# Two fused graph layers on one core: layer 0's masks kept on chip for layer 1, most loads moved to other steps and given one buffer

## The chip, the cores and the metric

The kernel runs on one core of a Trainium2 chip. A core has a matmul engine (PE, with its weight loads shown apart as PEld), a vector engine (DVE), a scalar engine (ACT), a general engine (POOL) and a queue processor (SP) that here only issues DMAs. Each of them works through its own list of instructions in order; a semaphore wait at the head of a list holds up everything behind it. Sixteen DMA engines move the data. The metric is the device time of one execution, in microseconds (us), lower is better.

## The reference

The input is `x`, 16 graphs of 1024 nodes with 256 features, and `adj`, 16 x 1024 x 1024 integers, here only zeros and ones (about 3% ones).

```
# layer 0: attention with 8 heads of 32, masked by adj == 0
h = relu(layernorm(x))
Q, K, V = h @ Wq.T + bq, h @ Wk.T + bk, h @ Wv.T + bv
scores = Q K.T * 32**-0.5, -inf where adj == 0
x = x + (softmax(scores) V) @ Wo.T + bo
# layer 1: one score per edge, by the kind of the edge (adj = 1, 2, 3, 4)
h = relu(layernorm(x))
e_k = leaky_relu((h * a_k) @ h.T, 0.2)
scores = e_0 where adj == 1, e_1 where adj == 2, ..., -9e15 elsewhere
x = x + softmax(scores) @ h
```

With an `adj` of zeros and ones, layer 1 needs e_0 alone. The kernel computes that case in its main loop, finds out on the way whether any graph has other values, and has a branch that computes layer 1 again for such a graph (`layer_1_of_kinds`, L597). With this input the branch is not entered.

## The kernel before, in words

The work is cut into 128 tiles: 16 graphs (b) of 8 tiles (t) of 128 rows. One pass of the main loop is a **step** s; it has eight parts, h = 0 to 7, one for each head of layer 0. Three kinds of objects are in flight:

- `Attend(b, t)` is layer 0 for one tile. In step s the object `now` has tile s: for each head h, `scores(h)` (PE, L402), `softmax_max(h)` (DVE, L414, adds the mask to the scores and finds the row's maximum), one part later `softmax_exp(h-1)` (ACT, L422), and one more part later the probabilities of head h-2 are turned over so that they can be multiplied by the values. For odd heads PE transposes and ACT copies (`turn`, L514, L515). For heads 0, 2, 4 and 6 (`BY_BLOCKS`) DVE transposes 32 x 32 blocks (`turn_blocks`, L347) and four DMAs of 128 KB put the blocks in place (`place_blocks`, that is `placed`, L352). `combine(0)` at h = 7 multiplies heads 0 to 3 by the values, `combine(1)`, at h = 3 of the next step (the object is then called `was`), heads 4 to 7 (PE, L457). So head 6's blocks, which are placed at h = 0, have to be in place by h = 3. I write place(6) for those four DMAs.
- `Edges(b, t)` is layer 1 for one tile, LAG = 9 steps behind layer 0. `prepare` (POOL, L530) scales a tile of h by a_0, `score(0)` and `score(1)` at h = 0 and 1 make the scores (PE, L543), `softmax_max` at h = 2 adds the mask and finds the maximum (DVE, L556), `leak`, `softmax_exp`, `turn_blocks` and `place_blocks` follow until h = 6, and in the step after that `gather` (PE, L584) and `store` (DVE, L593, and the DMA of the result).
- `Piece(b, t)` is layer 0's projection for a tile of the next graph, 9 steps ahead: load of x (`xin`, L192), layernorm statistics (`stats`, DVE, at h = 7), the scale by a Newton iteration on POOL (`scaled`, L144 to L160), `normed`, transposes, projections, and keys and queries written to DRAM (`kd`, `qd`). The main loop is preceded by a **start** that does this for the eight tiles of graph 0 with two large pieces of four tiles each, and for one small one.

What bears on the change:

- The mask. `Attend.mask` (POOL, L384, at h = 3 for the next tile) turns the 128 x 1024 integers into a bf16 tile `neg` with -1e30 where adj is 0. `Edges.mask` (POOL, L537, at h = 7 for the next tile) does the same from a second load of the same rows. Layer 0's load reads the rows in a "mixed" order over the partitions (`mixed`, L342: row 32b + k of the tile goes to partition 4k + b), which the block transposes make necessary; layer 1's load reads them in plain order. Each load is 512 KB.
- The flag. `Attend.flag` (ACT, L393) squares adj - 0.5 in place and sums, which tells whether there is anything but 0 and 1. It runs at h = 0 for the current tile and ends the use of the integers.
- The DMAs. SP issues nearly all of them in program order. In the order of a step: h = 0: keys of the piece (`kd`, L297), place(6); h = 1: `kd`, the next tile's adj (L376), the next tile's queries `qt` (L372); h = 2: place(0); h = 3: `xin` (L192), layer 1's adj (L525); h = 4: place(2), x1 for `store` (L572, issued in `Edges.softmax_exp`); h = 6: queries of the piece (`qd`, L291), place(4), `x1d` (L486, layer 0's result to DRAM), `xb` (L380, the residual's input), layer 1's four placing DMAs; h = 7: the result (L594). POOL issues a second copy of the keys at h = 1, and around a change of graph the eight loads of the next graph's keys, 512 KB each (`load_key`, L331): five in step t = 7 and three in step t = 0.
- `work.tile(...)` takes a buffer from a ring for its tag; the tags had two buffers unless told otherwise. A tile whose ring is full waits for the last reader of the oldest.

Of the kernel before, what the change touches and what calls it, by code (L numbers as in the profile page):

```python
# [8 lines left out]
F32 = mybir.dt.float32  # L9
# [33 lines left out]
def gnn_kernel(  # L43
# [25 lines left out]
    LAG = NT + 1  # L69
    LEAD = NT + 1  # L70

    const = ctx.enter_context(tc.tile_pool(name="const", bufs=1))
# [98 lines left out]
    class Piece:  # L171
# [5 lines left out]
        def __init__(self, b, first, n=1):  # L177
            self.b, self.first, self.n = b, first, n
            self.cols = slice(first * P, (first + n) * P)
            self.projected, self.halved, self.again = [], [], []  # L180
            self.tags = ("xin", "h0", "hT", "halves", "hTm") if n == 1 else ("adj", "pT", "qt", "p", "blocks")

        def buffer(self, i, shape, dtype=F32, bufs=2):
# [79 lines left out]
        def high(self):  # L263
            which, oc, ps, bias = self.projected.pop(0)
            halves = self.buffer(3, [P, 2 * self.n * P], F32R, 4)
# [91 lines left out]

    h1s, h1Ts, x1ds = {}, {}, {}
    kinds_seen = const.tile([P, B * NT], F32, name="kinds_seen")

    class Attend:


# [10 lines left out]
        def load(self):  # L374
            self.adj = work.tile([P, N], I32, tag="adj")
            nc.sync.dma_start(out=self.adj, in_=mixed(adj[self.b, self.rows, :]))  # L376

        def load_nodes(self):
            self.xb = work.tile([P, D], F32, tag="xb")
            nc.sync.dma_start(out=self.xb, in_=mixed(x[self.b, self.rows, :]))  # L380

        def mask(self):
            self.neg = work.tile([P, N], BF16, tag="neg")
            nc.gpsimd.tensor_scalar(self.neg, self.adj, 0.0, MASKED, ALU.is_equal, ALU.mult)  # L384
            self.sums = small.tile([P, HEADS], F32, tag="sums")
# [79 lines left out]
        def combined(self):  # L465
            self.oT = work.tile([P, NC, P], F32, tag="oT")
            nc.vector.tensor_tensor(self.oT, by_chunk(sums_place), self.recT, ALU.mult)
# [8 lines left out]
        def residual(self):  # L476
            self.x1 = work.tile([P, D], F32, tag="x1")
            nc.vector.tensor_tensor(self.x1, self.y, self.xb, ALU.add)
            mv = small.tile([P, 1, nc.vector.BN_AGGR_DIM], F32, tag="mv1")
            stats_of(self.x1, mv[:, 0, :])  # L480
            self.norm = norm_of(mv, 1, "1")

        def keep(self):
            if self.t == 0:
                x1ds[self.b] = dram.tile([N, D], F32, tag=f"x1d{self.b}", name=f"x1d_{self.b}", bufs=1)
            nc.sync.dma_start(out=mixed(x1ds[self.b][self.rows, :]), in_=self.x1)  # L486

# [30 lines left out]
    class Edges:  # L518
# [3 lines left out]

        def load(self):
            self.adj = work.tile([P, N], I32, tag="adj")
            nc.sync.dma_start(out=self.adj, in_=adj[self.b, self.rows, :])  # L525

        def prepare(self):
            self.ha = work.tile([P, NC, P], F32, tag="ha")
            for c in range(NC):
                nc.gpsimd.tensor_scalar(  # L530
                    self.ha[:, c], h1Ts[self.b][:, c, self.rows], a_t[:, c, 0:1], 0.0, ALU.mult, ALU.add
                )

        def mask(self):
            self.neg = work.tile([P, N], BF16, tag="neg1", bufs=1)

            nc.gpsimd.tensor_scalar(self.neg, self.adj, 0.0, MASKED, ALU.is_equal, ALU.mult)  # L537

# [12 lines left out]


        def softmax_max(self):
            self.sel = work.tile([P, N], F32, tag="sel", bufs=1)
            top = small.tile([P, 1], F32, tag="top")
            nc.vector.tensor_tensor_reduce(  # L556
                out=self.sel, in0=self.e, in1=self.neg, scale=-1.0, scalar=3e38,
                op0=ALU.add, op1=ALU.min, accum_out=top,
            )
            self.nmx = small.tile([P, 1], F32, tag="nmx1")  # L560
            nc.vector.scalar_tensor_tensor(self.nmx, top, SLOPE, top, ALU.mult, ALU.min)
# [4 lines left out]
        def softmax_exp(self):  # L566
# [3 lines left out]
            )  # L570
            self.x1 = work.tile([P, D], F32, tag="x1b")
            nc.sync.dma_start(out=self.x1, in_=x1ds[self.b][self.rows, :])  # L572
# [16 lines left out]
        def store(self):  # L589
            rec = small.tile([P, 1], F32, tag="rec1")  # L590
            nc.vector.reciprocal(rec, self.total)
            ot = work.tile([P, D], F32, tag="ot")
            nc.vector.scalar_tensor_tensor(ot, sums_place, rec, self.x1, ALU.mult, ALU.add)  # L593
            nc.sync.dma_start(out=out[self.b, self.rows, :], in_=ot)  # L594


    def layer_1_of_kinds(b):  # L597
        h1 = graph.tile([P, NT, D], F32, tag="h1", name=f"h1g_{b}")
        h1T = graph.tile([P, NC, N], F32, tag="h1T", name=f"h1Tg_{b}")
        for t in range(NT):  # L600
            rows = slice(t * P, (t + 1) * P)
            xt = work.tile([P, D], F32, tag="x1")
            nc.sync.dma_start(out=xt, in_=x1ds[b][rows, :])
            mv = small.tile([P, 1, nc.vector.BN_AGGR_DIM], F32, tag="mv1")
# [7 lines left out]
        for t in range(NT):  # L612
            rows = slice(t * P, (t + 1) * P)
            at = work.tile([P, N], I32, tag="adj")
            nc.sync.dma_start(out=at, in_=adj[b, rows, :])
            xt = work.tile([P, D], F32, tag="x1b")
            nc.sync.dma_start(out=xt, in_=x1ds[b][rows, :])

            code = work.tile([P, N], BF16, tag="neg1", bufs=1)
            nc.gpsimd.tensor_scalar(code, at, 5.0, 0.0, ALU.min, ALU.max)  # L620
            sel = work.tile([P, N], F32, tag="sel", bufs=1)
            nc.vector.memset(sel, NEG_INF)
            for k in range(N_KINDS):
                ha = work.tile([P, NC, P], F32, tag="ha")
# [4 lines left out]
                is_k = work.tile([P, N], U16, tag="neg")  # L629
                nc.vector.tensor_scalar(is_k, code, float(k + 1), None, ALU.is_equal)  # L630
# [21 lines left out]
            nc.vector.reciprocal(rec, total)  # L652
            ot = work.tile([P, D], F32, tag="ot")
            nc.vector.scalar_tensor_tensor(ot, o, rec, xt, ALU.mult, ALU.add)
# [19 lines left out]
    with tc.manual_schedule():  # L674
# [35 lines left out]
        for s in range(B * NT + LAG + 1):  # L710
            b, t = divmod(s, NT)
            nxt, edge_nxt, piece_nxt = attend_of(s + 1), edges_of(s + 1), piece_of(s + 1)
            for h in range(HEADS):
# [41 lines left out]
                if h == 0:  # L755
                    if edge:
                        edge.score(0)
                    if gone:
                        gone.turn_normed()
                        gone.turned_normed()  # L760
                    if now:
                        now.flag()
                if h == 1:
# [8 lines left out]
                    if nxt:  # L772
                        nxt.load()
                        nxt.load_queries()
# [28 lines left out]
                if h == 5:  # L803
# [37 lines left out]
                if now and h < 3 and t == 0 and b > 0:  # L841
                    load_key(b, HEADS - 3 + h)
            gone, was, now = was, now, nxt
            edge_was, edge = edge, edge_nxt
# [53 lines left out]
```

## Time and profile before

| | |
|---|---|
| time, median of 3 runs | 3405.14 us (3405.12 to 3412.75) |
| the profiled execution: its own time, its span | 3404.83 us, 3403.0 us |
| PE, DVE, ACT, POOL busy | 3126.6, 2788.1, 2418.2, 2432.1 us |
| mean granted PE clock | 0.978 |
| DMA | 830.24 MB, 244 GB/s on average |
| masks of layer 0 on POOL (L384) | 128 x 3653 ns |
| masks of layer 1 on POOL (L537) | 128 x 3659 ns |
| loads of adj, both layers | 256 of 512 KB, 5.3 us from issue to landing (median) |

A step in the middle of a graph takes about 24.6 us. "Idle before" an instruction is time in which its engine stood still, and the arrow names what ended it; the releaser is inferred, so that among several it can be a neighbour of the true one. The chain of work that ended last covers only the last 30 us of this run: it is followed back from the last instruction and breaks off where no releaser is recorded. Records of PE overlap, because matmuls are pipelined.

### The profile page before, as it was taken

The page shows a single profiled execution, that of the slowest core. Times are in us where ns is not written, and L with a number is a line of the kernel's source. Part 1 is how long each engine was busy: PE and PEld are TensorE (multiplying, and loading weights), DVE is VectorE, ACT ScalarE, POOL GpSimd, SP SyncE. Part 2 cuts the span into 40 slices and gives each one's busy share as a digit, 9 for nine tenths or more (in the row PEclk, how much of TensorE's full clock was granted, in tenths as well). Part 3 has the DMA queues.
Part 4 walks back from the last instruction along what each step waited for, and adds up shares of the span by engine and source line. Part 5 has one row for each costly group of instructions (what it writes and reads, how often), then busy time and mean ns, then how long its engine had stood idle before and what let it go on. Part 6 is the DMA issues. An engine that isn't in the chain of part 4 may idle for free. (4 is left out here: it accounts for less than half of the span.)

```text
span 3403.0 us, 100938 instructions
## 1 busy us (share of the span) xinstructions
PE 3126.6 (92%) x36018; PEld 2247.9 (66%) x36018; DVE 2788.1 (82%) x5111; ACT 2418.2 (71%) x4829; POOL 2432.1 (71%) x5634
## 2 busy tenths in 40 slices
PE   5879989999999989999899999999999999998988
PEld 3666767666676767766666676767666676666653
DVE  3878888788888888888788788888888888788874
ACT  2887767677777777777777677777777677776751
POOL 2567777777777777777777777777777777776553
PEclk7999999999999999999999999999999999999999
DMA  6787788888888788788878888888788888888664
GB/s 221 211 249 241 234 268 249 268 239 245 265 241 277 236 268 247 237 271 248 267 231 250 265 236 282 240 270 248 234 268 249 267 235 251 267 238 261 196 175 113
DMA packets 802029, 830.24 MB, mean 244 GB/s; under 512 B 73840, under 2 KB 742640, under 8 KB 801520
## 3 DMA queue, kind: packets, MB, share of 16 engines
q1 hardware_dynamic: 769520, 725.10, 71.3%
q0 software_dynamic: 28800, 94.39, 7.9%
q8 instruction: 291, 4.77, 0.5%
q10 hardware_dynamic: 3200, 4.19, 0.3%
q14 instruction: 218, 1.79, 0.1%
HBM read 320.08 MB, written 167.77 MB: 143 GB/s over the span
## 5 line engine op out<-in xcount | busy, mean ns | idle before, releaser
L422 ACT ACTIVATE p<-p,nmx 128x1024 f32<-128x1024 f32 x1024 | 1179.2, 1152 | 454.9 <-DVE nmx L414 450.9
L414 DVE CUSTOM_DVE_ANT_0 p<-s,neg 128x1024 f32<-128x1024 f32 x1024 | 1242.1, 1213 | 207.2 <-PE s L402 195.8
L402 PE MATMUL s<-k,qt 128*128 128x512 f32 x2048 | 794.5, 469 | 41.3 <-DMA k<-kd 14.8
L457 PE MATMUL acc<-pT,v 128*32 128x128 f32 x16384 | 576.3, 283 | 140.2 <-DMA pT<-blocks 136.6
L515 ACT COPY pT<-trp 128x512 f32<-128x512 f32 x1024 | 542.5, 580 | 136.1 <-PE trp L514 134.6
L347 DVE STREAM_TRANSPOSE blocks<-p 128x1024 f32<-128x1024 f32 x512 | 634.8, 1240 | 0.0
L457 PEld LDWEIGHTS acc<-pT,v 128*32 128x32 f32 x16384 | 476.1, 113 | 213.6 <-issue 204.4
L514 PE MATMUL trp<-ident,p 128*128 128x128 f32 x4096 | 534.0, 274 | 2.1 <-ACT p L422 2.0
L514 PEld LDWEIGHTS trp<-ident,p 128*128 128x128 f32 x4096 | 480.7, 141 | 75.1 <-ACT p L422 6.9
L384 POOL TENSOR_SCALAR neg<-adj 128x1024 bf16<-128x1024 int32 x128 | 467.6, 3653 | 78.8 <-DMA adj<-in_adj 69.8
L584 PE MATMUL acc<-h,pT 128*32 128x256 f32 x8192 | 505.8, 383 | 6.2 <-DMA pT<-blocks 5.5
L537 POOL TENSOR_SCALAR neg<-adj 128x1024 bf16<-128x1024 int32 x128 | 468.4, 3659 | 39.0 <-DMA adj<-in_adj 29.0
L402 PEld LDWEIGHTS s<-k,qt 128*128 128x128 f32 x2048 | 328.9, 191 | 232.0 <-issue 136.6
L543 PE MATMUL s<-h1T,ha 128*128 128x512 f32 x1024 | 481.3, 593 | 0.5 <-ACT h1T L504 0.5
L584 PEld LDWEIGHTS acc<-h,pT 128*32 128x32 f32 x8192 | 244.0, 110 | 219.3 <-issue 73.2
L156 POOL TENSOR_SCALAR sq<-sq 128x1 f32<-128x1 f32 (+1 forms) x750 | 238.6, 318 | 65.5
L441 POOL COPY wide<-rec 128x256 f32<-128x256 f32 x128 | 51.1, 399 | 325.7 <-DVE rec L439 325.6
L543 PEld LDWEIGHTS s<-h1T,ha 128*128 128x128 f32 x1024 | 183.9, 190 | 141.1 <-issue 127.5
L556 DVE CUSTOM_DVE_ANT_0 sel<-s,neg 128x1024 f32<-128x1024 f32 x128 | 156.7, 1224 | 134.8 <-POOL ve L144 85.4
L157 POOL TENSOR_TENSOR r<-r,sq 128x1 f32<-128x1 f32 (+1 forms) x750 | 168.8, 225 | 62.6
L297 POOL DMA_DIRECT2D kd<-halves x240 | 176.6, 773 | 33.9 <-issue 24.3
L422 ACT ACTIVATION_READ_ACCUMULATOR p<-p,nmx 128x1 f32 x1024 | 198.7, 194 | 0.0
(103 smaller groups left out, 4096.6 us busy)
## 6 DMA issues: line engine op xcount, KB each, us to landing
pT<-blocks SPq DMA_DIRECT2D x2560, 128.0 KB, 3.3
adj<-in_adj SPq DMA_DIRECT2D x256, 512.0 KB, 5.3
qt<-qd SPq DMA_DIRECT2D x128, 512.0 KB, 5.9
qd<-halves SPq DMA_DIRECT2D x240, 256.0 KB, 3.3
k<-kd POOLq DMA_DIRECT2D x120, 512.0 KB, 7.1
kd<-halves SPq DMA_DIRECT2D x240, 128.0 KB, 2.3
kd<-halves POOLq DMA_DIRECT2D x240, 128.0 KB, 5.3
xb<-in_x SPq DMA_DIRECT2D x128, 128.0 KB, 2.5
```

The source lines that it names most:

```text
L156: g.tensor_scalar(sq, sq, 1.5, None, ALU.add)
L347: nc.vector.transpose(blocks.rearrange("p b j q -> p j b q"), p)
L384: nc.gpsimd.tensor_scalar(self.neg, self.adj, 0.0, MASKED, ALU.is_equal, ALU.mult)
L402: nc.tensor.matmul(self.ps[:, cols], lhsT=self.qt[:, h, :], rhs=keysets[self.b][h][:, cols], start=True, stop=True,)
L414: nc.vector.tensor_tensor_reduce(out=p, in0=sides[h in (3, 5, 7)], in1=self.neg, scale=-SCALE, scalar=FLOOR, op0=ALU.add, op1=ALU.min, acc ...
L422: nc.scalar.activation(p, p, AF.Exp, bias=nmx, scale=-1.0, accum_out=self.sums[:, h : h + 1])
L457: nc.tensor.matmul(sums_place[r * HD : (r + 1) * HD, g * P : (g + 1) * P], lhsT=vs[self.b][:, j, place_of(h) : place_of(h) + HD], rhs=self ...
L514: nc.tensor.transpose(tr[:, j, :], p[:, jj * P : (jj + 1) * P], ident)
L515: copy(pT[:, half * 4 : half * 4 + 4, :], tr)
L537: nc.gpsimd.tensor_scalar(self.neg, self.adj, 0.0, MASKED, ALU.is_equal, ALU.mult)
L543: nc.tensor.matmul(self.e[:, cols], lhsT=self.ha[:, c, :], rhs=h1Ts[self.b][:, c, cols], start=(c == 0), stop=(c == NC - 1),)
L584: nc.tensor.matmul(sums_place[a * HD : (a + 1) * HD, :], lhsT=self.pT[:, j, a], rhs=h1s[self.b][:, j, :], start=(j == 0), stop=(j == NT - 1),)
```

## The change

The masks of layer 0 stay on chip in a ring of `KEPT = LAG + 1 = 10` buffers, and layer 1 reads the one of its tile: `Edges.load` and `Edges.mask` are gone. Since that mask has its rows in the mixed order, layer 1 now handles its rows in that order too: `prepare` permutes the columns of its weights as it scales them, x1 goes to DRAM and comes back in mixed order as it lies, and the result is stored through `mixed`. The branch for other kinds keeps the plain order (`in_order`).

The integers of layer 0 have one buffer instead of two. They are loaded two tiles ahead, at h = 7 (`nxt2.load`), after the flag of the next tile, which moves from h = 0 of its own step to h = 6 of the step before. `xin` moves from h = 3 to h = 5, x1 (`Edges.load_nodes`) from h = 4 of the step before to h = 0 of the step of `store`, `xb` from the step before the tile's own to h = 6 of the tile's own. Nearly all other tags get one buffer. The large pieces of the start take their x from the `pT` ring, not from `adj`, and the start now flags the first tile and loads the second.

```diff
+    KEPT = LAG + 1
-            self.tags = ("xin", "h0", "hT", "halves", "hTm") if n == 1 else ("adj", "pT", "qt", "p", "blocks")
+            self.tags = ("xin", "h0", "hT", "halves", "hTm") if n == 1 else ("pT", "pT", "qt", "p", "blocks")
-            bufs = {"p": 4, "blocks": 3}.get(tag, bufs)
+            bufs = {"p": 4, "blocks": 3, "halves": 4, "qt": 2}.get(tag, 1)
...
+    def in_order(rows):
+        return rows.rearrange("(k b) n -> b k n", b=NB)
     class Attend:
         def load(self):
-            self.adj = work.tile([P, N], I32, tag="adj")
+            self.adj = work.tile([P, N], I32, tag="adj", bufs=1)
...
         def mask(self):
-            self.neg = work.tile([P, N], BF16, tag="neg")
+            self.neg = work.tile([P, N], BF16, tag="neg", bufs=KEPT)
+            masks[self.b, self.t] = self.neg
...
         def keep(self):
-            nc.sync.dma_start(out=mixed(x1ds[self.b][self.rows, :]), in_=self.x1)
+            nc.sync.dma_start(out=x1ds[self.b][self.rows, :], in_=self.x1)
     class Edges:
-        def load(self):
-            self.adj = work.tile([P, N], I32, tag="adj")
-            nc.sync.dma_start(out=self.adj, in_=adj[self.b, self.rows, :])
         def prepare(self):
-                    self.ha[:, c], h1Ts[self.b][:, c, self.rows], a_t[:, c, 0:1], 0.0, ALU.mult, ALU.add
+                    self.ha[:, c].rearrange("p (k b) -> p k b", b=NB),
+                    h1Ts[self.b][:, c, self.rows].rearrange("p (b k) -> p k b", b=NB),
+                    a_t[:, c, 0:1], 0.0, ALU.mult, ALU.add,
-        def mask(self):
-            self.neg = work.tile([P, N], BF16, tag="neg1", bufs=1)
-            nc.gpsimd.tensor_scalar(self.neg, self.adj, 0.0, MASKED, ALU.is_equal, ALU.mult)
         def softmax_max(self):
-                out=self.sel, in0=self.e, in1=self.neg, scale=-1.0, scalar=3e38,
+                out=self.sel, in0=self.e, in1=masks[self.b, self.t], scale=-1.0, scalar=3e38,
...
         def store(self):
-            nc.sync.dma_start(out=out[self.b, self.rows, :], in_=ot)
+            nc.sync.dma_start(out=mixed(out[self.b, self.rows, :]), in_=ot)
...
         now, piece_next = attend_of(0), piece_of(0)
+        nxt = attend_of(1)
         now.load()
-        now.load_nodes()
         now.mask()
+        now.flag()
+        nxt.load()
         piece_next.load()
...  the main loop
                 if h == 0:
-                    if now:
-                        now.flag()
+                    if edge_was:
+                        edge_was.load_nodes()
                 if h == 1:
                     if nxt:
-                        nxt.load()
                         nxt.load_queries()
                 if h == 3:
-                    if piece_nxt:
-                        piece_nxt.load()
-                    if edge_nxt:
-                        edge_nxt.load()
                     if nxt:
                         nxt.mask()
                 if h == 5:
+                    if piece_nxt:
+                        piece_nxt.load()
                 if h == 6:
                     if was:
                         was.keep()
+                    if now:
+                        now.load_nodes()
                     if nxt:
-                        nxt.load_nodes()
+                        nxt.flag()
                 if h == 7:
-                    if edge_nxt:
-                        edge_nxt.mask()
+                    if nxt2:
+                        nxt2.load()
```

More of the change, by code (lines that the diff above doesn't have):

```diff
@@ L180, in __init__, with buffer @@
             self.projected, self.halved, self.again = [], [], []
-            self.tags = ("xin", "h0", "hT", "halves", "hTm") if n == 1 else ("adj", "pT", "qt", "p", "blocks")
-        def buffer(self, i, shape, dtype=F32, bufs=2):
+            self.tags = ("xin", "h0", "hT", "halves", "hTm") if n == 1 else ("pT", "pT", "qt", "p", "blocks")
+        def buffer(self, i, shape, dtype=F32):
             tag = self.tags[i]
@@ L264, in high @@
             which, oc, ps, bias = self.projected.pop(0)
-            halves = self.buffer(3, [P, 2 * self.n * P], F32R, 4)
+            halves = self.buffer(3, [P, 2 * self.n * P], F32R)
             order = "p (w t n) -> p w t n" if which == 0 else "p (t w n) -> p w t n"
@@ L355, in placed @@
         return pT.rearrange("p (a j q) -> p j a q", a=NB, j=NT)
-    h1s, h1Ts, x1ds = {}, {}, {}
+    h1s, h1Ts, x1ds, masks = {}, {}, {}, {}
     kinds_seen = const.tile([P, B * NT], F32, name="kinds_seen")
@@ L374, in load @@
         def load(self):
-            self.adj = work.tile([P, N], I32, tag="adj")
+            self.adj = work.tile([P, N], I32, tag="adj", bufs=1)
             nc.sync.dma_start(out=self.adj, in_=mixed(adj[self.b, self.rows, :]))
         def load_nodes(self):
-            self.xb = work.tile([P, D], F32, tag="xb")
+            self.xb = work.tile([P, D], F32, tag="xb", bufs=1)
             nc.sync.dma_start(out=self.xb, in_=mixed(x[self.b, self.rows, :]))
         def mask(self):
-            self.neg = work.tile([P, N], BF16, tag="neg")
+            self.neg = work.tile([P, N], BF16, tag="neg", bufs=KEPT)
+            masks[self.b, self.t] = self.neg
             nc.gpsimd.tensor_scalar(self.neg, self.adj, 0.0, MASKED, ALU.is_equal, ALU.mult)
@@ L465, in combined @@
         def combined(self):
-            self.oT = work.tile([P, NC, P], F32, tag="oT")
+            self.oT = work.tile([P, NC, P], F32, tag="oT", bufs=1)
             nc.vector.tensor_tensor(self.oT, by_chunk(sums_place), self.recT, ALU.mult)
@@ L476, in residual @@
         def residual(self):
-            self.x1 = work.tile([P, D], F32, tag="x1")
+            self.x1 = work.tile([P, D], F32, tag="x1", bufs=1)
             nc.vector.tensor_tensor(self.x1, self.y, self.xb, ALU.add)
@@ L521, in __init__ @@
             self.rows = slice(t * P, (t + 1) * P)
-        def load(self):
-            self.adj = work.tile([P, N], I32, tag="adj")
-            nc.sync.dma_start(out=self.adj, in_=adj[self.b, self.rows, :])
         def prepare(self):
-            self.ha = work.tile([P, NC, P], F32, tag="ha")
+            self.ha = work.tile([P, NC, P], F32, tag="ha", bufs=1)
             for c in range(NC):
                 nc.gpsimd.tensor_scalar(
-                    self.ha[:, c], h1Ts[self.b][:, c, self.rows], a_t[:, c, 0:1], 0.0, ALU.mult, ALU.add
-                )
-        def mask(self):
-            self.neg = work.tile([P, N], BF16, tag="neg1", bufs=1)
-            nc.gpsimd.tensor_scalar(self.neg, self.adj, 0.0, MASKED, ALU.is_equal, ALU.mult)
+                    self.ha[:, c].rearrange("p (k b) -> p k b", b=NB),
+                    h1Ts[self.b][:, c, self.rows].rearrange("p (b k) -> p k b", b=NB),
+                    a_t[:, c, 0:1], 0.0, ALU.mult, ALU.add,
+                )
         def score(self, nh):
@@ L570, in softmax_exp, with load_nodes @@
             )
-            self.x1 = work.tile([P, D], F32, tag="x1b")
+        def load_nodes(self):
+            self.x1 = work.tile([P, D], F32, tag="x1b", bufs=1)
             nc.sync.dma_start(out=self.x1, in_=x1ds[self.b][self.rows, :])
@@ L591, in store @@
             nc.vector.reciprocal(rec, self.total)
-            ot = work.tile([P, D], F32, tag="ot")
+            ot = work.tile([P, D], F32, tag="ot", bufs=1)
             nc.vector.scalar_tensor_tensor(ot, sums_place, rec, self.x1, ALU.mult, ALU.add)
-            nc.sync.dma_start(out=out[self.b, self.rows, :], in_=ot)
+            nc.sync.dma_start(out=mixed(out[self.b, self.rows, :]), in_=ot)
     def layer_1_of_kinds(b):
@@ L601, in layer_1_of_kinds @@
             rows = slice(t * P, (t + 1) * P)
-            xt = work.tile([P, D], F32, tag="x1")
-            nc.sync.dma_start(out=xt, in_=x1ds[b][rows, :])
+            xt = work.tile([P, D], F32, tag="x1", bufs=1)
+            nc.sync.dma_start(out=xt, in_=in_order(x1ds[b][rows, :]))
             mv = small.tile([P, 1, nc.vector.BN_AGGR_DIM], F32, tag="mv1")
@@ L613, in layer_1_of_kinds @@
             rows = slice(t * P, (t + 1) * P)
-            at = work.tile([P, N], I32, tag="adj")
+            at = work.tile([P, N], I32, tag="adj", bufs=1)
             nc.sync.dma_start(out=at, in_=adj[b, rows, :])
-            xt = work.tile([P, D], F32, tag="x1b")
-            nc.sync.dma_start(out=xt, in_=x1ds[b][rows, :])
-            code = work.tile([P, N], BF16, tag="neg1", bufs=1)
+            xt = work.tile([P, D], F32, tag="x1b", bufs=1)
+            nc.sync.dma_start(out=xt, in_=in_order(x1ds[b][rows, :]))
+            code = work.tile([P, N], BF16, tag="neg", bufs=KEPT)
             nc.gpsimd.tensor_scalar(code, at, 5.0, 0.0, ALU.min, ALU.max)
@@ L623, in layer_1_of_kinds @@
             for k in range(N_KINDS):
-                ha = work.tile([P, NC, P], F32, tag="ha")
+                ha = work.tile([P, NC, P], F32, tag="ha", bufs=1)
                 for c in range(NC):
@@ L628, in layer_1_of_kinds @@
                     )
-                is_k = work.tile([P, N], U16, tag="neg")
+                is_k = work.tile([P, N], U16, tag="neg", bufs=KEPT)
                 nc.vector.tensor_scalar(is_k, code, float(k + 1), None, ALU.is_equal)
@@ L652, in layer_1_of_kinds @@
             nc.vector.reciprocal(rec, total)
-            ot = work.tile([P, D], F32, tag="ot")
+            ot = work.tile([P, D], F32, tag="ot", bufs=1)
             nc.vector.scalar_tensor_tensor(ot, o, rec, xt, ALU.mult, ALU.add)
@@ L711, in gnn_kernel @@
             b, t = divmod(s, NT)
-            nxt, edge_nxt, piece_nxt = attend_of(s + 1), edges_of(s + 1), piece_of(s + 1)
+            nxt2, edge_nxt, piece_nxt = attend_of(s + 2), edges_of(s + 1), piece_of(s + 1)
             for h in range(HEADS):
@@ L842, in gnn_kernel @@
                     load_key(b, HEADS - 3 + h)
-            gone, was, now = was, now, nxt
+            gone, was, now, nxt = was, now, nxt, nxt2
             edge_was, edge = edge, edge_nxt
```

## The prediction

> **What bounds the kernel now.** I read the page's totals first, then the chain, the list of waits, the DMA queue's own waits, and then the timeline of single steps, engine by engine. The chain covers only the last 30 us, so it says nothing of the steps. The totals:
>
> ```profile
> PE 3126.6 (92%) x36018; PEld 2247.9 (66%) x36018; DVE 2788.1 (82%) x5111; ACT 2418.2 (71%) x4829; POOL 2432.1 (71%) x5634
> L537 POOL TENSOR_SCALAR neg<-adj 128x1024 bf16<-128x1024 int32 x128 | 468.4, 3659 | 39.0 <-DMA adj<-in_adj 29.0
> ```
>
> POOL, which the change relieves most (468 us), stands idle 29% of the time. The list of waits (who, for what: us in total, times, longest) says what that relief could pay:
>
> ```profile
> PE acc L457 <- DMA pT<-blocks: 136.6, 111, 5.3
> POOL neg L384 <- DMA adj<-in_adj: 69.8, 25, 7.6
> DVE sel L556 <- POOL neg L537: 10.6, 5, 5.9
> SPq L352 <- DVE rec L591: 172.7, 126, 8.2
> ```
>
> Only 10.6 us of DVE in the run waited for a mask that goes. The large wait is PE's, in combine(1), for place(6). The last line is SP's own: once a step it waits, and what releases it is DVE's head-4 transpose, which ends as L591 begins. The timeline of SP after that, in one step (start, length):
>
> ```profile
> 1720.99 2.54 SPq L352 DMA_DIRECT2D pT<-blocks  x4
> 1723.58 0.62 SPq L486 DMA_DIRECT2D x1d<-x  x1
> 1724.30 0.56 SPq L380 DMA_DIRECT2D xb<-in_x  x1
> 1724.95 2.50 SPq L352 DMA_DIRECT2D pT<-blocks  x4
> 1727.55 0.54 SPq L594 DMA_DIRECT2D out<-ot  x1
> 1728.19 0.55 SPq L297 DMA_DIRECT2D kd<-halves  x1
> 1728.83 2.53 SPq L352 DMA_DIRECT2D pT<-blocks  x4
> 1731.46 0.56 SPq L297 DMA_DIRECT2D kd<-halves  x1
> 1732.12 0.58 SPq L376 DMA_DIRECT2D adj<-in_adj  x1
> ```
>
> From place(4) to place(6) SP issues without a pause; head 6's transpose is ready at 1727.76, and place(6) starts at 1728.83 because SP comes no sooner. Its DMAs land 2.6 us after issue. PE and DVE around combine(1):
>
> ```profile
> 1709.40 1.94 PE L457 MATMUL acc<-pT,v 128*32 128x128 f32 x60 [0.26 <-DMA pT<-blocks]
> 1712.27 1.16 PE L253 MATMUL acc<-hTm,wqT 128*128 128x128 f32 x8 [0.27 <-DVE v L326]
> 1730.36 1.22 DVE L556 CUSTOM_DVE_ANT_0 sel<-s,neg 128x1024 f32<-128x1024 f32 x1 [0.91 <-POOL ve L144]
> ```
>
> So two loops set the step. Loop 1, one step long: PE runs unbroken from L253 to the end of layer 1's scores (1712.27 to 1730.25; L556 waits for these, not for POOL), DVE from L556 to L326 (1736.67), which lets the next L253 go at 1736.73: 24.46 us. Loop 2, two steps long: combine(1) at 1709.40, L556 at 1730.36 (20.96), place(4) at 1745.44 (15.08), combine(1) two steps on at 1758.21 (12.77): 48.81, or 24.40 a step. They are level. Where both waits occur in a step they add up to 0.53 us: a wait for place(6) beyond 0.53 delays PE, one below is given back at L253. Read step by step, of the 104 steps with layer 1 that are not the first of a graph 57 waited longer (0.97 on average), 36 less (0.37), 11 not at all. The 14 first steps of a graph waited 4.35 on average, with eight key loads in the queues.
>
> **The change part by part.** The sum is made against the profiled execution's own 3404.83 us (span 3403.0 and 1.8 around it), which is 0.3 below the median.
>
> *Masks of layer 1 gone*, 128 x 3.66 us on POOL: POOL's list ends each step with that mask and then idles (4.96 us before L441 at 1705.13, 2.04 a step later) until DVE's L439. Of the 10.6 us above, 5.9 lie in the tail behind layer 0, where PE's score ends 0.2 before the mask does; the rest are four first steps of a graph that wait for place(6) right after. I take -2 us, between 0 and -5. The tail's steps (8.7 us) are a chain of score, softmax, placing and gather in which the mask is done before L556; nothing there.
>
> *The new wait of a kept mask's buffer*: `mask` at h = 3 waits for L556 at h = 2 of the same step, ended at 1707.1, while POOL reaches it at 1714.27. Nothing. Were it late, `prepare` and `scaled` behind it would be.
>
> *Loads of layer 1's adj gone*, 512 KB and an SP issue (0.45 us) a step at h = 3: SP is idle there, and the DMA engines, full from 1711 to 1715, are full for nobody who waits. Nothing in a middle step.
>
> *Layer 0's adj moved to h = 7*: it passes, on SP, from behind place(6) to between `out` and `kd`, that is into the unbroken run ahead of place(6). Its issue takes 0.58 and a gap of 0.07. So place(6) starts and lands 0.65 us later in every step. Loop 2 grows by 0.65 per two steps: 57 x 0.65/2 = 18.5; 36 x (0.65 - 0.16)/2 = 8.8, 0.16 being what was left of 0.53; the 11 without a wait nothing; 14 first steps 4.6. Sum 32 us. Lower end: loop 1 hides it, 0. Upper end: the 512 KB delay place(6) too, as the queue moves them first. At 349 GB/s, the rate when full, they take 1.5 us. But the engines are 71 to 77% busy there:
>
> ```profile
> 1720.00:1727.00 7.00, 7.00 (x99) 5.23 (x92) 5.19 (x11) 4.41 (x9) 5.85 (x15) 1.00 0.71 209
> 1727.00:1733.00 6.00, 6.00 (x38) 4.59 (x36) 5.03 (x12) 5.00 (x10) 3.10 (x13) 1.00 0.77 209
> 1872.00:1889.00 17.00, 11.42 (x114) 7.76 (x112) 12.22 (x22) 12.26 (x25) 14.71 (x37) 0.98 1.01 349
> ```
>
> (The stretch of time, its length, the five engines' busy time, granted PE clock, DMA share, GB/s.) The load's own issue slot covers 0.65 of the 1.5, and five slots that leave a quarter free, 0.16 each, the rest. With all 1.5 instead of 0.65 the same working gives 57 x 0.75 + 36 x 0.67 + 14 x 0.75 = 77 us. I take 0.65, since the share is what place(6) runs beside. Here the Trainium skill's "DMA: Bandwidth & Descriptors" (Queues, rings and completion order; Anatomy of one DMA) speaks against the move: an engine consumes a ring in order, and data moves at 436 GB/s, so 512 KB put ahead cost 1.2 us, by which the term would be some 60 us.
>
> *First steps of a graph*: DMA is full from 1872 to 1889, as the third line shows. The moved load costs up to 1.5 us more there, the load gone at h = 3 of the step before takes up to 1.5 away if the backlog reaches back that far. I take these as cancelling; 14 x 1.5 = 21 us either way stay in the range.
>
> *Flag from h = 0 to h = 6*, 1.34 us of ACT: it delays head 6's exponential from 1719.87 to 1720.3; ACT's 1.17 us of idle before the copies at 1722.27 hides that. It also waits for POOL's mask (ends 1717.93; ACT is there at 1719.05). Without that cover the copies and L493 behind them slip by what POOL is late.
>
> *xin at h = 5, single buffer*: issued where x1 was (1717.46, 3.5 us to land), read by DVE's statistics at 1722.99, behind which max(0) waits 1.1 us for PE anyway. Nothing; bound 14 x 1 us, where x1 took 6.3. *x1, xb*: still a part or more ahead of their readers; on SP x1 takes, behind place(6), the slot adj leaves. *`prepare` permuted*: 0.73 a step; doubled, it delays L493 by 0.7 and PE needs that 2.3 later. *Other single buffers*: each is rewritten after its last reader's part. The skill's "Trainium Kernel Development and Optimization" (Best Practices) asks for double buffers so that loads overlap compute; by it the 5.3 us of each adj load would show in each step, some 680 us, but the row has mask L384 four parts behind the load.
>
> *Start*: new on ACT between `normed` and the first copy is the flag, which waits for POOL's mask:
>
> ```profile
> 33.27 1.05 ACT L227 COPY qt<-trn 128x512 f32<-128x512 f32 x2
> 32.80 3.67 POOL L384 TENSOR_SCALAR neg<-adj 128x1024 bf16<-128x1024 int32 x1
> ```
>
> The mask ends at 36.47, the flag at 37.8, so the copy and all behind it come 4.5 us later. The first adj load, no longer behind the large pieces, doesn't help: POOL reaches the mask after three `scaled`. Between +3 and +5.
>
> Sum: 32 + 4.5 - 2 = +34.5, that is 3404.8 + 34.5 = 3439 us.
>
> **The rivals.** *Faster (0.16)*: loop 1 hides the slot, and at the 14 graph changes the halved adj traffic shortens place(6)'s wait by 1.5 us each: 3405 + 4.5 - 21 - 5 = 3384. For it: DMA share 1.01 there; against: the moved load stands in the same queue. It decides when a middle step loses less than 0.2 us (21 us over 104). *Hidden (0.17)*: place(6) is late, but DVE keeps loop 1 the longer: 3405 + 4.5 and up to 8, 3405 to 3417. For it 24.46 against 24.40; against it the 57 steps beyond 0.53. *Heavier (0.17)*: the 512 KB delay place(6) in full, and PE's longer halts lower its clock, as at 1888 to 1895 where it was granted 0.5: 3405 + 77 + 4.5 = 3487. For it the ring order; against it the share of 0.75. *The change doesn't do what it says*: masks still made or loaded twice; the diff leaves no second load, so this is left out. My forecast has 0.5, its own range 3422 to 3456.
>
> **How the numbers follow.** The range of 3390 to 3482 takes in the main case, the hidden one and about half of both outer ones. A measurement of this kernel can tell about 0.3% (10 us) from no change. Faster by more: the first rival less its edge, 0.14. Within: most of the hidden case, 0.13. Slower: the rest, 0.73.
>
> **What would show it.** L537 and 128 loads gone, POOL near 1960 us busy. SP's unbroken run shows adj between `out` and `kd`; place(6) starts 8.5 instead of 7.84 us after place(4), combine(1)'s wait for pT<-blocks rises from 136.6 us to 160 or more, and middle steps from 24.6 to 24.9. The copy L227 starts near 37.8. The prediction is wrong if middle steps stay at 24.6, if xin becomes a wait of DVE, or if first steps of a graph (29.6 us) move by more than 1.5.

## The result, and the profile after

The change makes the kernel slower: 3625.39 us (3622.68 to 3636.19) against 3408.94 us for the kernel before on the same chip. That is 1.0636 times as long, 95% interval 1.0602 to 1.067. The forecast was 3439 us, its range ended at 3482. The sign was right; the loss is 216 us where 34 were forecast.

The totals, and two groups of instructions, of the kernel after (busy time, mean ns of one, idle time before them and its releaser):

```profile
span 3620.8 us, 100886 instructions
PE 3190.3 (88%) x36018; PEld 2335.8 (65%) x36018; DVE 2792.6 (77%) x5111; ACT 2449.0 (68%) x4829; POOL 1994.9 (55%) x5506
L464 PE MATMUL acc<-pT,v 128*32 128x128 f32 x16384 | 657.4, 307 | 328.5 <-DMA pT<-blocks 324.7
L474 DVE TENSOR_TENSOR oT<-acc,recT 128x256 f32<-128x256 f32 x128 | 54.2, 423 | 231.7 <-PE acc L464 198.9
```

POOL has lost its 437 us and the kernel is no better for it. PE does the same 36018 matmuls and is busy 64 us longer; the mean granted clock fell from 0.978 to 0.949. L464 is combine, L457 before. The list of waits of the kernel after (who, for what: us, times, longest):

```profile
PE acc L464 <- DMA pT<-blocks: 324.7, 129, 8.5
DVE oT L474 <- PE acc L464: 198.9, 95, 9.1
SPq L357 <- DVE rec L594: 182.4, 124, 8.8
DVE st L166 <- DMA xin<-in_x: 8.3, 7, 1.7
```

The first line was 136.6 us in 111 waits. The second is the news: DVE now waits 198.9 us for combine(1). The list of waits of the kernel before has that line too, small, and the prediction had passed over it:

```profile
DVE oT L467 <- PE acc L457: 23.4, 22, 5.4
```

By the times at which oT is made, one per step (before, after, us; the stretch from the first scores to the first oT and the last 8 us of the span are left out):

| | before | after |
|---|---|---|
| first scores of layer 0 start | 69.5 | 73.3 |
| 9 early steps, sum | 203.6 | 209.9 |
| 82 steps in the middle of a graph, mean | 24.70 | 26.64 |
| 14 last steps of a graph, mean | 24.67 | 26.93 |
| 14 first steps of a graph, mean | 31.54 | 31.47 |
| 8 late steps, sum | 185.9 | 206.4 |
| from the last oT to the last instruction of DVE | 91.0 | 89.6 |

The loss sits in every ordinary step, 1.9 to 2.3 us in each. The timeline of SP in one such step after (start, length):

```profile
1859.19 2.53 SPq L357 DMA_DIRECT2D pT<-blocks  x4
1861.76 0.60 SPq L493 DMA_DIRECT2D x1d<-x  x1
1862.46 0.55 SPq L386 DMA_DIRECT2D xb<-in_x  x1
1863.11 2.50 SPq L357 DMA_DIRECT2D pT<-blocks  x4
1865.71 0.60 SPq L597 DMA_DIRECT2D out<-ot  x1
1866.41 1.47 SPq L382 DMA_DIRECT2D adj<-in_adj  x1
1867.97 0.56 SPq L298 DMA_DIRECT2D kd<-halves  x1
1868.62 2.56 SPq L357 DMA_DIRECT2D pT<-blocks  x4
```

The run is the one foreseen, with adj between `out` and `kd`. Place(6) starts 9.43 us after place(4); 0.9 of that is this adj issue being a long one (1.47 us, where the median of the 128 is 0.56). The step with 7.84 us that the prediction read was a short one: by the median over 127 steps the distance was 8.46 us before and is 9.31 after. What follows on PE and DVE (in brackets the idle time before, and its releaser):

```profile
1873.94 3.56 PE L464 MATMUL acc<-pT,v 128*32 128x128 f32 x60 [2.33 <-DMA pT<-blocks]
1877.62 0.42 DVE L474 TENSOR_TENSOR oT<-acc,recT 128x256 f32<-128x256 f32 x1 [2.94 <-PE acc L464]
```

The matmuls that took 1.94 us before take 3.56 here, and DVE stands still until they are done. The windows of that step, just ahead of the matmuls and in them (length, busy time of the five engines, granted PE clock, DMA share, GB/s):

```profile
1870.00:1873.90 3.90, 1.61 (x14) 1.08 (x12) 3.90 (x5) 2.52 (x5) 3.01 (x11) 1.00 1.00 336
1873.94:1875.80 1.86, 1.86 (x36) 1.73 (x40) 0.75 (x3) 1.35 (x3) 0.18 (x1) 0.50 0.53 138
```

After a halt of 2.33 us PE is granted half its clock. The DMA share ahead of the matmuls is 1.00, where the prediction counted on a quarter left free. Lastly what the DMA engines moved while SP issued place(6), 2.6 us in the next step of the kernel after; packets and bytes, then the DMAs issued there and their median time from issue to landing:

```profile
DMA packets 128, 0.50 MB, mean 194 GB/s; under 512 B 1, under 2 KB 6, under 8 KB 128
pT<-blocks SPq DMA_DIRECT2D x4, 128.0 KB, 3.9
kd<-halves SPq DMA_DIRECT2D x1, 128.0 KB, 4.2
```

and the same for the step of the kernel before that the prediction showed:

```profile
DMA packets 702, 0.52 MB, mean 201 GB/s; under 512 B 65, under 2 KB 702, under 8 KB 702
pT<-blocks SPq DMA_DIRECT2D x4, 128.0 KB, 2.6
kd<-halves SPq DMA_DIRECT2D x1, 128.0 KB, 2.3
```

Before, the engines moved small packets, the blocks and keys. After, 0.50 MB in 128 packets, nearly all of 2 KB and more: these are the rows of adj, and the blocks behind them have to wait. They land 3.9 us after their issue instead of 2.6. The same holds over the whole run: the median of the DMAs of place(6) is 3.68 us after and 2.60 before, and from the issue of the first of the four to the landing of the last it is 5.25 us after and 4.55 before.

**The loop.** After the change the steps follow a loop that is one step long and that the prediction did not have. Combine(1) on PE gives DVE its `oT`. DVE works in order, so all that stands behind oT in its list, head 4's transpose among it, comes no sooner. That releases place(4), x1d and the rest of SP's run, at its end place(6), and place(6) lets the next combine(1) go. Its three legs, in us, are means over the 96 middle and last steps of the table; combine(1) counts from the 60 matmuls behind the wait:

| | combine(1) starts to oT | oT to the issue of x1d | x1d to the next combine(1) | sum |
|---|---|---|---|---|
| before | 2.43 | 11.76 | 10.51 | 24.70 |
| adj_back (below) | 2.27 | 11.74 | 10.63 | 24.64 |
| slot_small (below) | 2.35 | 11.89 | 11.40 | 25.64 |
| slot_full (below) | 2.82 | 12.04 | 11.96 | 26.82 |
| pe_busy (below) | 2.06 | 11.85 | 11.84 | 25.75 |
| after | 2.81 | 11.97 | 11.91 | 26.69 |

Each leg begins where the last one ends, so they add up to a step in any case. What shows that the loop sets the step are the waits (of more than 0.15 us). After the change DVE waits for combine(1) at oT, and PE waits for place(6) in combine(1), in all 96 of these steps. Before, PE waited for place(6) in 87 of them, but DVE for combine(1) in 11 alone: in the others DVE came to oT later than that, and the loop had a few tenths of slack in its first leg (2.43 us, where 2.06 are enough in pe_busy). The theory that the experiments test: the whole loss is the place of the adj load; its issue and its transfer both delay place(6), the delay beyond this slack counts in full in every step, and it makes PE's halt long enough that the clock falls, which counts as well.

### The profile page after: what moved, and what is told of

Its sections match the earlier page's. It is cut to its first block, busy times and chain, and to the rows that moved or that the text cites. A ratio compares the mean times of both kernels' runs of the same rounds, so it can differ in the third digit from the quotient of the medians.

```text
span 3620.8 us, 100886 instructions
## 1 busy us (share of the span) xinstructions
PE 3190.3 (88%) x36018; PEld 2335.8 (65%) x36018; DVE 2792.6 (77%) x5111; ACT 2449.0 (68%) x4829; POOL 1994.9 (55%) x5506
## 5 line engine op out<-in xcount | busy, mean ns | idle before, releaser
L464 PE MATMUL acc<-pT,v 128*32 128x128 f32 x16384 | 657.4, 307 | 328.5 <-DMA pT<-blocks 324.7
L409 PE MATMUL s<-k,qt 128*128 128x512 f32 x2048 | 808.2, 476 | 25.2 <-DVE nmx L421 16.3
L464 PEld LDWEIGHTS acc<-pT,v 128*32 128x32 f32 x16384 | 544.0, 123 | 407.1 <-issue 309.1
L391 POOL TENSOR_SCALAR neg<-adj 128x1024 bf16<-128x1024 int32 x128 | 471.1, 3681 | 38.5 <-DMA adj<-in_adj 24.6
L157 POOL TENSOR_SCALAR sq<-sq 128x1 f32<-128x1 f32 (+1 forms) x750 | 266.8, 356 | 65.5
L474 DVE TENSOR_TENSOR oT<-acc,recT 128x256 f32<-128x256 f32 x128 | 54.2, 423 | 231.7 <-PE acc L464 198.9
L511 ACT COPY h1T<-acc 128x256 f32<-128x256 f32 x128 | 47.6, 372 | 214.1 <-PE acc L507 214.1
```

The source lines that it names most:

```text
L157: g.tensor_scalar(sq, sq, 1.5, None, ALU.add)
L409: nc.tensor.matmul(self.ps[:, cols], lhsT=self.qt[:, h, :], rhs=keysets[self.b][h][:, cols], start=True, stop=True,)
L464: nc.tensor.matmul(sums_place[r * HD : (r + 1) * HD, g * P : (g + 1) * P], lhsT=vs[self.b][:, j, place_of(h) : place_of(h) + HD], rhs=self ...
```

## Experiments

All of them change the order or the amount of work alone. None leaves out any of the computation; what slot_small, slot_full, pe_busy and short_busy add is read by nobody. The kernel before ran beside each of them: 3400.92 us for the first four, 3402.72 us for start_late, run_short and run_short_h7, 3399.68 us for the other two.

**adj_back**: the kernel after, with adj's load back behind place(6).

```diff
-        nxt.load()                             # in the start
...  the main loop
                 if h == 1:
                     if nxt:
+                        nxt.load()
                         nxt.load_queries()
...
                 if h == 7:
-                    if nxt2:
-                        nxt2.load()
```

> The changed kernel with one thing undone: layer 0's adj is loaded at h = 1 again, behind place(6), for the next tile only (one buffer, the flag stays at h = 6, all else stays changed). Theory R (the run): all of the loss but the start comes from the load standing in SP's run ahead of place(6). Then middle steps take 24.3 to 24.8 us and the time is 3395 to 3425 us. Theory P (other parts: single buffers, xin at h = 5, the permuted weights, the flag at h = 6): middle steps stay near 26.6 and the time is 3580 or more.

Measured: 3394.66 us, ratio 0.9973 (0.9952 to 0.9993). Middle steps take 24.64 us again, first scores start at 73.3 as in the kernel after. Its list of waits:

```profile
PE acc L464 <- DMA pT<-blocks: 146.6, 108, 6.0
DVE oT L474 <- PE acc L464: 33.4, 38, 7.9
```

So one moved DMA is the whole loss of some 230 us. Kept masks, single buffers, the moved flag, the mixed order and the start together cost nothing that can be told: they gain a little. The rival theory, that the single buffers or the permuted `prepare` did it, falls.

**slot_small** and **slot_full** split the load into its issue and its transfer. Both are adj_back with another DMA in the place that adj's load had at h = 7: one of 8 KB (16 rows of 512 bytes), and one that copies adj's 512 KB from DRAM to DRAM.

```diff
+        def spare(self):                       # slot_small
+            s = work.tile([P, 128], I32, tag="spare", bufs=1)
+            nc.sync.dma_start(out=s[:16], in_=adj[self.b, self.t * P : self.t * P + 16, 0:128])
+        def spare(self):                       # slot_full
+            s = dram.tile([P, N], I32, tag="spare", name="spare")
+            nc.sync.dma_start(out=s, in_=mixed(adj[self.b, self.rows, :]))
...
                 if h == 7:
+                    if nxt2:
+                        nxt2.spare()
```

> adj_back with an extra DMA of 8 KB (16 rows of 512 bytes, read by nobody) where the change put the adj load, between out and kd: an issue slot on SP with next to no transfer. Theory R splits the loss into slot (0.65 us), transfer (about 1.0 us, from place(6) landing 3.6 us after issue where it took 2.6) and PE's clock. With the slot alone place(6) starts 0.65 us later, lands 2.6 to 2.7 us after issue, combine(1) waits under 2 us in most steps, and the time is 10 to 60 us above adj_back. The forecast's own theory, slot alone matters, says 30 us above adj_back here and as much with a full transfer. Theory P says no difference.

> adj_back with an extra DMA of 512 KB in that place (the same adj rows, 4 KB each, copied to a DRAM buffer that nobody reads). Theory R: place(6) lands 3.4 to 3.8 us after issue, waits of combine(1) pass 2 us, the matmuls behind them run at a lower clock, and the time comes to 3570 to 3650 us, near the changed kernel. The forecast's theory: as slot_small, some 3440 us. Theory P: as adj_back.

Measured: slot_small 3504.29 us, ratio 1.0304 (1.0266 to 1.0341); slot_full 3647.91 us, ratio 1.0695 (1.065 to 1.074). Their waits, slot_small's first:

```profile
PE acc L468 <- DMA pT<-blocks: 249.8, 124, 6.1
DVE oT L478 <- PE acc L468: 108.7, 96, 7.5
```

```profile
PE acc L468 <- DMA pT<-blocks: 325.9, 123, 8.8
DVE oT L478 <- PE acc L468: 213.6, 101, 8.3
```

The bare slot of an issue costs 110 us over adj_back, more than the 60 at which my expectation ended. By the median, place(6) starts 9.20 us after place(4) instead of adj_back's 8.55: 0.65, one issue with its gap. The leg from x1d to combine(1) grew by 0.77 us and middle steps by 0.97 on average. A loop two steps long would have lengthened the step by half of the delay; here the step grew by more than the delay. The clock takes its share in that: waits over 1.9 us rose from 18 to 49. With the full transfer place(6) starts no later (9.27), but its DMAs land 3.75 us after their issue instead of 2.62; the leg is 11.96, 0.56 more than slot_small's, waits over 1.9 us are 94, and the time is 144 us above slot_small. So slot and transfer both count. slot_full is some 20 us slower than the kernel after: beside this copy it still moves adj_back's own load in each step.

**pe_busy** takes the clock by itself: the kernel after, with twelve 128 x 128 transposes of the identity ahead of combine(1), so that PE has work in part of the halt.

```diff
+        def idle_work(self):
+            spare = by_chunk(brief)
+            for i in range(12):
+                nc.tensor.transpose(spare[:, i % NC, :], ident, ident)
...
                     if was:
+                        was.idle_work()
                         was.combine(1)
```

> The changed kernel with 12 transposes of the identity (0.13 us each, 1.5 us in all, into a PSUM place that is free then and read by nobody) put ahead of combine(1), so that PE works through most of its wait. Theory C (a wait of about 2 us costs PE its clock, and the slow matmuls behind it are part of the loss): the 60 matmuls of combine(1) take 1.94 us again where they took 2.9 on average, and the time falls by 50 to 150 us, to 3475 to 3575 us. If the clock has no part: no gain, 3610 to 3660 us.

Measured: 3536.14 us, ratio 1.0401 (1.0369 to 1.0434), 89 us below the kernel after, with 1536 more instructions on PE. Its group of combine and its wait:

```profile
L464 PE MATMUL acc<-pT,v 128*32 128x128 f32 x16384 | 570.4, 280 | 164.0 <-DMA pT<-blocks 157.2
PE acc L464 <- DMA pT<-blocks: 157.2, 111, 9.1
```

PE is busy 87 us less in combine (657.4 us in the kernel after), the mean granted clock is 0.981, where it was 0.978 before the change. The leg from x1d to combine(1) is 11.84 us, the kernel after has 11.91, so the blocks come about as late as there; the leg from combine(1) to oT is 2.06 instead of 2.81. Over the 96 middle and last steps that is 72 of the 95 us between the two profiled executions; most of the rest is the middle leg (12 us) and the late steps (10 us). The two ran on different chips; by their ratios to the kernel before (1.0636 and 1.0401) the gain is 80 us. The idle transposes have a cost of their own in this number, which no run separates.

This run also shows the length of the loop with the clock taken out. Against adj_back the leg from x1d to combine(1) is 1.21 us longer and the step 1.11: the delay less the 0.21 of slack, with 0.11 more in the middle leg, and not half of it.

**start_late**: adj_back with the first tile's flag behind the projections of the start.

```diff
         now.mask()
-        now.flag()
...
+        now.flag()
...  the main loop
```

> adj_back with the start's flag put behind the projections of the start, where ACT has nothing to wait for. If the flag in front of the first copies is what made the first scores come 3.8 us later (73.3 instead of 69.5 us), they come at 69.5 to 70 again and the time falls by 3 to 4 us against adj_back, to about 3391 us. If the start is held by something else (x of the large pieces in the pT ring), the first scores stay at 73.

Measured: 3390.42 us, ratio 0.9968 (0.9951 to 0.9984). First scores start at 69.1 instead of 73.3, so the start's term was right. In the whole time 4 us are too little to tell this ratio from adj_back's.

**run_short** turns the finding round. If each DMA in SP's run costs its slot in every step, then three others, x1d, xb and the result, belong behind place(6) as well (kernel: start_late with this edit).

```diff
+        def send(self):                        # the DMA of store, now by itself
+            nc.sync.dma_start(out=mixed(out[self.b, self.rows, :]), in_=self.ot)
...
                 if h == 0:                     # behind place(6)
+                    if was:
+                        was.load_nodes()
+                    if gone:
+                        gone.keep()
+                    if edge_gone:
+                        edge_gone.send()
...
                 if h == 6:
-                    if was:
-                        was.keep()
-                    if now:
-                        now.load_nodes()
```

> start_late with SP's run ahead of place(6) made shorter: x1d, xb and the result's DMA are issued behind place(6), at h = 0 of the next step, so that only place(4), layer 1's placing and kd are left in it. Theory R, with the loop of one step (combine(1), then oT on DVE, place(4), the run, place(6), combine(1)): the run loses 1.9 us, of which 1.0 can show, as head 6's transpose is then the later one; the loop falls from 24.5 to 23.5 us, the other loop (24.46) sets the step, waits of combine(1) shrink, and middle steps fall by 0.1 to 0.3 us, first steps of a graph by 0.5 to 1.5: 15 to 45 us less than start_late, some 3350 to 3375 us. If the step is set by PE and DVE alone: no change beyond 5 us.

Measured: 3340.85 us, ratio 0.9829 (0.9807 to 0.9852). Its wait for place(6) is nearly gone:

```profile
PE acc L464 <- DMA pT<-blocks: 44.3, 20, 3.8
```

Middle steps are 24.48 us on average, first steps of a graph 29.1 instead of 31.0. The gain, 50 us on start_late, is larger than expected; most of it (27 us) lies in the 14 first steps, not in the middle ones.

**run_short_h7**: run_short with adj's load at h = 7, where the change has it.

> run_short with the adj load where the change put it, at h = 7 ahead of place(6) and two tiles ahead. Theory R: the slot is paid by the shorter run, since place(6) then starts with head 6's transpose, and only the transfer (1.0 us on place(6)'s landing, perhaps less as fewer DMAs surround it) is left: 0 to 70 us above run_short, so 3355 to 3440 us, where the same load cost 231 us in the changed kernel. If the load does its harm elsewhere (queries, flag, POOL), it costs about 230 us here too.

Measured: 3357.13 us, ratio 0.9874 (0.9852 to 0.9896). The same move that cost some 230 us costs 16 here, 14 first steps of a graph taking 30.53 instead of 29.1 us. Where place(6) has slack, the slot and the transfer are free.

**before_short**: the kernel before with only those three DMAs moved; masks made twice and two buffers as before.

> The kernel before with nothing of the change, but with x1d, xb and the result's DMA behind place(6) as in run_short (adj loads at h = 1 and h = 3, two buffers, masks made twice). Theory R: the length of SP's run is what counts and the kept masks next to nothing, so it comes within 20 us of run_short: 3335 to 3365 us. If the kept masks, or 67 MB less to move, carry a part of run_short's gain of 62 us, it stays at 3370 to 3400.

Measured: 3369.28 us, ratio 0.992 (0.9899 to 0.9941), just short of the gain expected. Its wait for place(6) is as short as run_short's (38.4 us, 23 times). So the short run alone brings 0.8%, and with the kept masks and the later flag of the start 1.7%. The rest of the change is worth something once SP's run is short. Four us of that are the start. The larger part is in the middle steps (24.74 against 24.48 on average) and in the first steps of a graph (29.51 against 29.1); what makes it was not settled.

**short_busy**: run_short, with pe_busy's twelve transposes in the first step of each graph alone.

```diff
+                        if was.t == NT - 1:
+                            was.idle_work()
                         was.combine(1)
```

> run_short with the 12 idle transposes ahead of combine(1), but in the first step of each graph only, where combine(1) still waits 2 us or more. Theory C: its 60 matmuls take 1.94 us there again where they took 2.5 to 2.9, 14 times 0.6 to 1.0: 5 to 15 us less than run_short. If the clock has no part: 0 to 10 us more.

Measured: 3329.99 us, ratio 0.98 (0.9777 to 0.9822), mean granted clock 0.994. Its wait:

```profile
PE acc L464 <- DMA pT<-blocks: 18.7, 14, 1.9
```

No wait for place(6) exceeds 1.9 us now, and the matmuls behind them all take 1.94 us. By the median it is the fastest of all, 2% below the kernel before and 8% below the kernel after. The 11 us against run_short are what theory C expected, but the intervals of the two ratios overlap, so that the time alone does not show the gain.

## Why the prediction was right or wrong

- *The steps that were named right.* The load goes from behind place(6) into SP's unbroken run and takes about 0.65 us of it (slot_small: 0.65). That the distance from place(4) would be 8.5 us was read from one short step; the median went from 8.46 to 9.31. All of the loss comes from there (adj_back).
- *Wrong: "Loop 2, two steps long", and with it "0.65 / 2" a step.* The loop through place(6) is one step long, through oT and DVE's order. The working followed layer 1's L556 back to PE and did not ask what DVE itself waits for behind combine(1); the line that says so (23.4 us for oT) was in the list of waits. That line was small because the loop still had slack in most steps; a delay of 0.65 us was more than the slack. In slot_small the slot takes 0.77 us in the leg, per step.
- *Wrong: "I take 0.65, since the share is what place(6) runs beside", the transfer at nothing.* A mean share of 0.71 to 0.77 tells of bytes, not of order: the rows of adj are moved first, and in the window shown the engines are then full (1.00) up to combine(1). The transfer costs 0.56 us a step by the leg (slot_full less slot_small) and 0.70 by the landing of the last of the four DMAs (5.25 less 4.55). The Trainium skill's "DMA: Bandwidth & Descriptors" (Queues, rings and completion order), which spoke against the move, was nearer: the order in the ring is what the packets above show. The 1.2 us for 512 KB, the prediction's estimate from the page's 436 GB/s, is above both.
- *Wrong: PE's clock had no price in the main case.* It stood in the rival "Heavier" as an aside, with a place but no size. In the kernel after, the 60 matmuls behind a wait of combine(1) took 1.94 us when the wait was below 1.5, on average 2.12 at 1.5 to 2, 2.82 at 2 to 2.5, 3.09 at 2.5 to 3. Waits over 1.9 us: 18 before, 93 after. This is worth 80 to 89 us (pe_busy).
- *The sum by these terms.* Against adj_back a step of the kernel after is 2.05 us longer by the means. The leg from x1d to combine(1) has 1.28 of it: 0.77 that the slot alone takes in slot_small, the rest the transfer. The leg from combine(1) to oT has 0.54: 0.75 of clock by pe_busy, less the 0.21 of slack. The middle leg has 0.23, half of it gone again in pe_busy. Over 96 steps that is 197 us, and the early and late steps lost 27 more; between the two profiled executions lie 226.
- *The rival Heavier* named both mechanisms that came true, but its price, 77 us, used the two-step working too. *Hidden* and *Faster* fall: a middle step lost 1.9 us, not less than 0.2.
- *Right: the other terms, taken as nothing or next to it.* The masks gone, the kept mask's buffer, the single buffers, the flag at h = 6 and the permuted `prepare` (0.73 us before, 0.97 after on POOL) show no cost: adj_back has all of them at 0.9973. The first steps of a graph moved by 0.07 us, within the 1.5 allowed. xin at h = 5 did become a wait of DVE, which the prediction had named as a sign of being wrong; it was 8.3 us in 7 steps, inside the bound of 14; adj_back keeps xin at h = 5 and has none.
- *Right: the start,* 3.8 us for the 4.5 taken, POOL 1994.9 us busy for the 1960 forecast.

## What to carry to other kernels

When an engine with an in-order list waits for a result, everything behind it in that list is part of the loop: follow each loop through the lists, not only through the data, and count its length in steps before halving a delay. A queue's unbroken run of issues ahead of a late transfer is a place to take DMAs out of, and the last one in which to put a large one: its slot and its bytes both delay what follows. A wait that grows past a point can cost more than itself, here because PE's clock falls.

## What the runs showed of the hardware that was not expected

- PE's clock falls after short halts. After one of 2.33 us it was granted 0.50 at once, and waits of 2 to 2.5 us already cost 0.9 us in the 1.94 us of matmuls behind them. In the kernel after, the clock was at 0.5 during these matmuls behind 32 of 46 waits of 2 to 2.5 us, behind 4 of 27 of 1.5 to 2 us, and behind none of the shorter ones. The Trainium skill's "TensorE: Matmul & The Clock Gate" (HAM oscillation — how this bites in real kernels) puts the limit at idle gaps of more than some 3.4 us. The measurement decides: here the clock begins to fall at waits near 2 us, and not at a sharp limit. What the gate counts, no run tells.
- Twelve transposes that nobody reads, 1536 in the run, make the kernel after 80 to 89 us faster when they fill part of such halts.
- An 8 KB DMA takes as much of SP's run as one of 512 KB (0.60 and 0.56 us an issue), and it cost 110 us here (slot_small). Now and then an issue takes 0.9 to 1.2 us longer (x1d 1.83, adj 1.47); what causes it was not looked into.
